# Attention and feed-forward block: the two 1024x1024 layers on 1024 tokens at a time instead of 512, after attention and the gated layer of all tokens

## The chip, the cores and the metric

The kernel runs on one core of one Trainium2 chip. The metric is device time in microseconds; the time shown is the median of three runs. A separate, profiled execution gives the trace that all the rows below come from. Its span runs from the first to the last instruction, and its own measured time is a little longer than its span.

## The reference, cut to what matters

Input x has 8 batches of 256 rows of 256 numbers; ctx has 120 rows of 256 for each batch.

```python
x = x + xattn(layernorm(x), ctx, ctx, ctx)     # h = gelu(xn @ ctx.T) * (xn @ ctx.T); h @ ctx
x = x + ffn(layernorm(x))

def ffn(x):                                    # weights are -1, 0 or 1, one scale per output column
    h = silu(tlin(x, w1)) * tlin(x, w2)        # 256 -> 1024, twice
    h = gelu(tlin(h, h1))                      # 1024 -> 1024
    h = gelu(tlin(h, h2))                      # 1024 -> 1024
    return tlin(h, w3)                         # 1024 -> 256
```

All numbers are 32 bit floats. There are 2048 token rows in all.

## The kernel before, in words

**Data.** Activations lie with features on the 128 partitions and tokens along the free side. A layer's 1024 features are two halves of 512 (four blocks of 128). The large operands are split into a rounded high part and a low part (the rest), both in the type float32r, so each product is done twice, once with each part. The weights are small integers and exact.

**Tokens.** The 2048 tokens are four groups of 512, t = 0 to 3; each has two batches (c = 0, 1).

**Attention** (class `Attention`, lines 179 to 278) works on one batch: layernorm (statistics L224, aggregates L228, epsilon L229, power -0.5 on GpSimd L232, normalization on VectorE L236), four transposes (L248), scores (L253), Gelu built from a square, a tanh and two VectorE steps (L266 to L271), values (L258), residual x1 (L274), a second layernorm, four transposes, and the split into xT high and low (L386, L387). It has three sets of buffers.

**Gated layer** (`gated`, L395): for each of eight feature blocks eight matmuls (L406), a Silu (L428) and a multiply (L430). For t = 0 it is done in two halves of 256 tokens, otherwise with 512-column matmuls.

**Hidden layers** (`hidden`, L470): a 1024x1024 layer on 512 tokens is treated as a 2x2 by 2x2 block product with seven block products instead of eight (Winograd's form of Strassen's method). The blocks of the activations are two feature halves by two batches, 512 features by 256 tokens each. `combine` (L473) forms the differences of blocks on VectorE, `operand` (L443) splits a block into high (ScalarE, L455) and low (VectorE, L459), and each product is 32 matmuls of 256 columns (L488). Sums of products are formed partly in PSUM, partly by copies (L508) and adds (L513), then Gelu (L498). Four of the seven weight blocks are loaded; `sum_weights` (L340) forms the sums.

**Stages.** Attention of batches 0 and 1 comes first; then, for each t, the gated layer and the first hidden layer, with the attention of the next group between the products. The results of the first layer for t = 0, 1, 2 go to DRAM (`spill`, L642) and are fetched again (L651) for the second layer, which runs for t = 3, 0, 1, 2, with the output layer (`output`, L543) of a finished group between the products of the next. Residual rows x1 of all batches stay in SBUF. The second layer's weights have tiles of their own, which take the place of the gated layer's weights. The last steps are row scaling and residual (L281, L282) and the transfer of 128 rows (L560).

**Check.** Each loaded weight is compared with its rounded form on the side: a Sign on ScalarE (L353), an accumulating transfer on GpSimd's queue (L355) and an OR on VectorE (L357). A flag selects a general path that this input doesn't take.

**Order.** All steps are put into a list with an engine, an estimated duration and the keys that they read and write. `Plan` orders them by a list schedule: the ready step with the longest remaining chain goes first, with ranks altered by random draws whose seeds are listed in `PICKS`. The order on each engine is then fixed in the program. Matmuls of the products stay in program order among themselves (chain "main"), as do those of the output ("out"), and the weight loads on GpSimd's queue ("weights"). Plain loads and stores go through SP's queue.

Of the kernel before, what the change touches and what calls it, by code (L numbers as in the profile page):

```python
# [20 lines left out]
P = 128  # L21
NB = 8
# [9 lines left out]
RING = 4  # L32

PICKS = (
    22, 45, 50, 74, 104, 131, 164, 176, 201, 234, 250, 272, 301, 336, 451, 637, 985, 1048, 1076,
    1087, 1162, 1188, 1253, 1293, 1302, 1322, 1348, 1410, 1437, 1496, 1527, 1586, 1637, 1766,
    1800, 1916, 2021, 2155, 2228, 2261, 2374, 2518, 2712, 2767, 2934, 2972, 3083, 3173, 3226,
    3393, 3456, 3487, 3595, 3625, 3738, 3967, 3987, 4030, 4260, 4277, 4303, 4438, 4471, 4529,
    4557, 4631, 4753, 4792, 4821, 5029, 5162, 5277, 5281, 5943, 6311, 6315, 6360, 6825, 6957,
    7038, 7141, 7325, 7506, 11104, 11302, 14059, 14203, 14339, 14562, 14820, 16005, 35431,  # L40
    35629, 36277, 36481, 37244, 38287, 38876, 40840, 40973, 59388, 59602, 59975, 60086, 60142,
    60267,
)
FORCE_GENERAL = False

# [10 lines left out]
GROUP = {2: "a", 1: "b", 6: "b", 7: "b", 4: "b", 5: "c", 3: "c"}  # L56
BANKS = {"a": (0, 1), "c": (2, 3), "b": (4, 5)}
OPENS, CLOSES = (1, 5, 2), (2, 3, 4)
ORDER = (1, 5, 2, 6, 3, 7, 4)
ORDER_FIRST = (1, 2, 5, 6, 3, 7, 4)  # L60
ORDER_NEXT = (1, 5, 6, 3, 7, 2, 4)
# [99 lines left out]
PE = 0.119  # L161
# [3 lines left out]
def xattn_ffn_kernel(ctx: ExitStack, tc: tile.TileContext, x, ctx_b, wall, scal, s3, out):  # L165
# [13 lines left out]
    class Attention:  # L179


        def __init__(self, pool, n):
            new = lambda name, shape: [pool.tile(shape, F32, name=f"{name}{i}") for i in range(n)]
            self.xb, self.cb = new("xb", [P, 2, D]), new("cb", [P, 2 * L + D])
            self.xn, self.xnT = new("xn", [P, 2, D]), new("xnT", [P, 2, S])
            self.e, self.q = new("ge", [L, S]), new("gq", [L, S])
            self.st, self.mv = new("ln_st", [P, 2, 6]), new("ln_mv", [P, 2, 2])
            self.ve, self.rs = new("ln_ve", [P, 2]), new("ln_rs", [P, 2])

        def load(self, plan, b, i, pieces):  # L190
            xv = x[b * S : (b + 1) * S, :].rearrange("(j p) d -> p j d", p=P)

            def load_x(js):
                nc.sync.dma_start(self.xb[i][:, js, :], xv[:, js, :])  # L194

            for js in pieces:
                plan.dma("SP", 0.45, lambda js=js: load_x(js), 0.128 * (js.stop - js.start),
                         lag=(2.2, 3.5)[b] if b < 2 else 8.0, w=[("xb", i, j) for j in range(js.start, js.stop)])
            plan.dma("SP", 0.45, lambda: nc.sync.dma_start(self.cb[i], ctx_b[b]), 0.25,
                     lag=2.5 if b < 2 else 8.0, w=[("cb", i)])  # L200

        def run(self, plan, b, i, js, bank, bank_key, x1, x1_key, finish, early):
# [6 lines left out]
            keys = lambda name: [(name, i, j) for j in blocks]  # L209
            xb, xn = self.xb[i][:, js, :], self.xn[i][:, js, :]  # L210
            cT = self.cb[i][:, : 2 * L].rearrange("p (k l) -> p k l", k=2)
            cN = self.cb[i][:L, 2 * L :]
            xnT, e, q = self.xnT[i][:, :, cols], self.e[i][:, cols], self.q[i][:, cols]
            st, mv = self.st[i][:, js, :], self.mv[i][:, js, :]
            ve, rs = self.ve[i][:, js], self.rs[i][:, js]
# [5 lines left out]
            def layernorm(src, src_keys, name):  # L221
# [4 lines left out]
                def aggregate():  # L226
                    for j in range(nj):
                        nc.vector.bn_aggr(mv[:, j, :], st[:, j, :])  # L228
                    nc.vector.tensor_scalar_add(ve, mv[:, :, 1], EPS)  # L229

                def root():
                    nc.gpsimd.tensor_tensor(rs, ve, eps_exp[:, :nj], op=ALU.pow)  # L232

                def norm():
                    for j in range(nj):
                        nc.vector.tensor_scalar(  # L236
                            xn[:, j, :], src[:, j, :], mv[:, j, 0:1], rs[:, j : j + 1],
                            op0=ALU.subtract, op1=ALU.mult)

                add("DVE", 0.42 * nj, stats, src_keys, keys("st"))  # L240
                add("DVE", 0.17 * nj + 0.15, aggregate, keys("st"), keys("mv"))
                add("POOL", 0.45 + 0.3 * nj, root, keys("mv"), keys("rs") + [(name, b, j) for j in blocks])
                add("DVE", 0.42 * nj, norm, src_keys + keys("mv") + keys("rs"), keys("xn"))
# [20 lines left out]
            add("PE", 0.43 * nj, scores, keys("xnT") + [("cb", i)], [bank_key])  # L264
# [8 lines left out]
            add("PE", 0.43 * nj, values, keys("e") + [("cb", i)], [bank_key])  # L273
# [11 lines left out]
    with ExitStack() as es, ExitStack() as wide:  # L285
# [4 lines left out]
        dram = open_pool(es, "spill", space=DRAM)  # L290
        es.enter_context(tc.manual_schedule())

        mm = [psum.tile([P, N], F32, name=f"mm{i}") for i in range(6)]
        pa = [psum.tile([P, N], F32, name=f"pa{i}") for i in range(2)]
        hi = [keep.tile([P, 4, S], F32R, name=f"hi{i}") for i in range(RING)]
        lo = [keep.tile([P, 4, S], F32R, name=f"lo{i}") for i in range(RING)]
        half = {n: keep.tile([P, 4, N], F32, name=n) for n in ("hb0", "hb1", "hc0", "hc1")}
        p1 = keep.tile([P, 4, S], F32, name="p1")
        u2 = keep.tile([P, 4, S], F32, name="u2")
        p5 = keep.tile([P, 4, S], F32, name="p5")  # L300
        x1 = keep.tile([P, 2 * NB, D], F32, name="x1")
        spill = dram.tile([NT, 2, P, 4 * N], F32, name="spill")

        first = es.enter_context(ExitStack())
        h1p = open_pool(first, "h1p")
        h1 = {n: h1p.tile([P, 4, 4, P], F32R, name=f"h1_{n}")
              for n in ("11", "12", "21", "22", "s1", "s2", "s4")}
        early_pool = open_pool(wide, "early", side="right")
        w12 = early_pool.tile([P, 4, 1024], F32R, name="w12")
        xT = [early_pool.tile([P, 2, N], F32R, name=f"xT{i}") for i in range(2)]  # L310
        att = Attention(early_pool, 3)

        def rings_of(pool, into):
            into["d"] = [pool.tile([P, 1024], BF16, name=f"d{i}") for i in range(4)]
            into["w32"] = pool.tile([P, 2, 512], F32, name="w32")

        sooner, later = {}, {}
        rings_of(early_pool, sooner)
# [10 lines left out]
        def load_layer(layer, blocks, order, gate=()):  # L329
            for name in order:  # L330
                plan.dma("POOL", 0.8, lambda name=name: nc.gpsimd.dma_start(
                    blocks()[name].rearrange("p m k c -> p m (k c)"), block_rows(layer, name)), 1.05 * (1 + 0.5 * layer),
                         r=gate, w=[("h", layer, name, m) for m in range(4)], chain="weights")

        def sum_weights(layer, blocks):
            for into, a, b, op in (("s1", "21", "22", ALU.add), ("s2", "s1", "11", ALU.subtract),
                                   ("s4", "12", "s2", ALU.subtract), ("21", "11", "21", ALU.subtract)):
                for m in range(4):
                    add("DVE", dve(512), lambda into=into, a=a, b=b, op=op, m=m:
                        nc.vector.tensor_tensor(  # L340
                            blocks()[into][:, m], blocks()[a][:, m].bitcast(F32),
                            blocks()[b][:, m].bitcast(F32), op=op),
                        r=[("h", layer, a, m), ("h", layer, b, m)], w=[("h", layer, into, m)])
# [3 lines left out]
        def check(of, tile, src, keys, rings, gate=()):  # L347

            d = lambda i=checks[0] % 4: rings()["d"][i]
            key = ("d", checks[0] % 4)  # L350
            checks[0] += 1
            d4 = lambda: d().rearrange("p (m c) -> p m c", m=src.shape[1])
            add("ACT", act(1024), lambda: nc.scalar.activation(  # L353
                d(), tile().bitcast(F32), AF.Sign, scale=-1.0), r=keys + list(gate), w=[key])
            plan.dma("POOL", 0.8, lambda: nc.gpsimd.dma_start(d4(), src, accum_op=ALU.add), 1.04,  # L355
                     w=[key], lag=8.0)
            add("DVE", 0.16 + 512 / 960, lambda: nc.vector.tensor_tensor(  # L357
                bad, bad, d(), op=ALU.logical_or), r=[key], w=["bad"])

        def check_block(layer, blocks, name, rings, gate=()):  # L360
            for m in (0, 2):
                src = block_rows(layer, name)[:, m : m + 2, :]
                if name != "21":
                    keys = [("h", layer, name, m), ("h", layer, name, m + 1)]
                    tile = lambda m=m: blocks()[name][:, m : m + 2].rearrange("p m k c -> p (m k c)")
                else:
                    keys = ["w32"]
                    tile = lambda: rings()["w32"].rearrange("p m c -> p (m c)")
                    plan.dma("SP", 0.45, lambda src=src: nc.sync.dma_start(rings()["w32"], src), 0.52,
                             r=gate, w=["w32"], lag=6.0)  # L370
                check(name, tile, src, keys, rings, gate)

        def check_chunk(c, tile, keys, rings, gate=()):
            check(c, tile, wall[c : c + 1].rearrange("c p f -> p c f"), keys, rings, gate)


        def attention(b, pieces, banks, early):
            t, c, i = b // 2, b % 2, b % 3
            att.load(plan, b, i, pieces)
            for js, (bank, key) in zip(pieces, banks):  # L380
                cols = slice(c * S + js.start * P, c * S + js.stop * P)
                xkey = [("xT", c, j) for j in range(js.start, js.stop)]

                def finish(p, bank_key, n, early, cols=cols, xkey=xkey):
                    hi, lo = (v[:, :, cols] for v in xT)
# [402 lines left out]
```

## Time and profile before

| | |
|---|---|
| median of 3 runs | 350.26 us (349.5 to 350.3) |
| profiled execution, its own time | 350.58 us |
| its span | 348.8 us |
| TensorE, VectorE, ScalarE, GpSimd busy | 331.8, 266.0, 224.0, 46.9 us |
| hidden products, share of the chain | 61.2% (1792 matmuls of 256 columns) |
| gated layer, share of the chain | 17.2% (192 of 512 columns, 128 of 256) |
| output layer, share of the chain | 8.6% (256 of 256 columns) |

In the chain of work that ended last each piece has its start, its duration, its engine, the tile that it writes, its line and the number of instructions. In the groups a row has the line, the engine, the operation, the tiles and shapes, the count, the busy time, the mean duration of one and the idle time before it. A matmul's own duration in such a row (284 ns with 256 columns) includes time that overlaps with the next one; what one costs in a dense stretch is the stretch divided by its count.

### The profile page before, as it was taken

To read this page: it belongs to the slowest core of one execution; us is meant where nothing else is said; L and a number is where in the kernel's file an instruction comes from. 1 tells how busy PE (TensorE), PEld (TensorE's weight loads), DVE (VectorE), ACT (ScalarE), POOL (GpSimd) and SP (SyncE) were. 2 spreads that over 40 slices of the span, in tenths; PEclk is the share of its full clock that TensorE was granted. 3 is DMA by queue.
4 is the path that set the end of the run, shared out by engine and by line. 5 is a ranking of instruction groups with operands and counts; after the bars stand their busy time and mean duration, and the time that the engine had idled before them with its cause. 6 is when DMAs were issued, how large, how long until landed. Compare 5 with 4: busy or idle time off the path is not lost.

```text
span 348.8 us, 6241 instructions
## 1 busy us (share of the span) xinstructions
PE 331.8 (95%) x2502; PEld 317.7 (91%) x2502; DVE 266.0 (76%) x440; ACT 224.0 (64%) x360; POOL 46.9 (13%) x57
## 2 busy tenths in 40 slices
PE   3799999999999999999999999999999999999991
PEld 2499999888999889999899999999999999999991
DVE  4779998878988678952598998999499846895551
ACT  2339566697974968456585588989487636854540
POOL 5411000261423100000040005105000000000000
PEclk9999999999999999999999999999999999999998
DMA  7992001599596620004149917715780006000011
GB/s 201 375 381 81 2 0 34 150 291 156 47 138 62 185 85 2 2 2 165 77 131 400 314 62 79 116 19 56 94 274 32 1 17 257 15 17 31 20 43 37
DMA packets 19042, 38.81 MB, mean 111 GB/s; under 512 B 1472, under 2 KB 10816, under 8 KB 17472
## 3 DMA queue, kind: packets, MB, share of 16 engines
q0 software_dynamic: 10256, 17.30, 26.9%
q1 hardware_dynamic: 8752, 21.06, 16.9%
q8 instruction: 21, 0.34, 0.4%
q14 instruction: 13, 0.11, 0.1%
HBM read 35.73 MB, written 8.39 MB: 126 GB/s over the span
## 4 chain that ended last, share of the span: by engine, by line
PE 94%; DVE 2%; DMA 1%; ACT 1%; issue 0%; SPq 0%
PE mm L488 61%; PE mm L406 17%; PE pa L543 9%; PE pa L258 2%; PE pa L253 2%; PE pa L248 2%; DMA sc<-scal_d 1%; PE mm L258 1%; PE mm L253 1%; DVE xT L387 0%; DVE o L281 0%; PE mm L248 0%; SPq L194 0%; DVE gq L267 0%; ACT ge L266 0%
## 5 line engine op out<-in xcount | busy, mean ns | idle before, releaser
L488 PE MATMUL mm<-hi,h 128*128 128x256 f32 x512 | 72.4, 284 | 0.0
L488 PE MATMUL mm<-lo,h 128*128 128x256 f32 x512 | 71.4, 282 | 0.0
L488 PEld LDWEIGHTS mm<-hi,h 128*128 128x128 f32 x512 | 65.7, 190 | 0.5 <-ACT hb L428 0.3
L488 PEld LDWEIGHTS mm<-lo,h 128*128 128x128 f32 x512 | 65.6, 190 | 0.0
L406 PE MATMUL mm<-xT,w 128*128 128x512 f32 (+1 forms) x320 | 63.0, 355 | 0.8 <-ACT xT L386 0.7
L406 PEld LDWEIGHTS mm<-xT,w 128*128 128x128 f32 x320 | 52.2, 194 | 9.1 <-ACT xT L386 1.0
L459 DVE TENSOR_TENSOR lo<-hb,hi 128x1024 fp32r<-128x1024 f32 (+2 forms) x47 | 52.5, 1129 | 7.6 <-ACT hi L455 7.4
L488 PE MATMUL mm<-hi,h_s 128*128 128x256 f32 x384 | 54.2, 284 | 0.0
L488 PE MATMUL mm<-lo,h_s 128*128 128x256 f32 x384 | 53.5, 282 | 0.0
L455 ACT CAST hi<-hb 128x1024 fp32r<-128x1024 f32 (+2 forms) x47 | 45.3, 975 | 7.5 <-issue 2.5
L488 PEld LDWEIGHTS mm<-hi,h_s 128*128 128x128 f32 x384 | 49.3, 190 | 0.2
L488 PEld LDWEIGHTS mm<-lo,h_s 128*128 128x128 f32 x384 | 49.2, 190 | 0.0
L498 ACT ACTIVATE hc<-hc,sc 128x256 f32<-128x256 f32 x60 | 27.3, 504 | 15.8 <-DVE hc L513 15.8
L355 POOL DMA_DIRECT2D d<-wall_d x22 | 24.8, 1141 | 93.3 <-ACT d L353 90.9
L430 DVE SCALAR_TENSOR_TENSOR hb<-hb,sc,mm 128x512 f32<-128x512 f32 (+1 forms) x40 | 25.1, 637 | 13.9 <-ACT hb L428 9.9
L428 ACT ACTIVATE hb<-mm,sc 128x512 f32<-128x512 f32 (+1 forms) x40 | 23.7, 604 | 15.2 <-PE mm L406 15.0
L232 POOL TENSOR_TENSOR ln_rs<-ln_ve,eps_exp 128x2 f32<-128x2 f32 (+1 forms) x18 | 13.8, 798 | 92.5 <-DVE ln_ve L229 51.8
L508 ACT COPY p<-mm 128x512 f32<-128x512 f32 x32 | 18.5, 585 | 10.0 <-PE mm L488 9.6
L459 DVE TENSOR_TENSOR lo<-hc,hi 128x1024 fp32r<-128x1024 f32 x18 | 21.8, 1219 | 2.5 <-ACT hi L455 2.5
L455 ACT CAST hi<-hc 128x1024 fp32r<-128x1024 f32 x18 | 18.8, 1048 | 4.9 <-DVE hb L513 2.3
L543 PE MATMUL pa<-w,hi 128*128 128x256 f32 x128 | 21.5, 281 | 0.4 <-DVE o L281 0.4
L543 PE MATMUL pa<-w,lo 128*128 128x256 f32 x128 | 21.1, 279 | 0.0
(85 smaller groups left out, 387.7 us busy)
## 6 DMA issues: line engine op xcount, KB each, us to landing
h<-wall_d POOLq DMA_DIRECT2D x8, 1024.0 KB, 14.6
spill<-hc SPq DMA_DIRECT2D x6, 1024.0 KB, 4.3
d<-wall_d POOLq DMA_DIRECT2D x22, 256.0 KB, 5.9
w<-wall_d POOLq DMA_DIRECT2D x3, 1024.0 KB, 9.9
w<-wall_d SPq DMA_DIRECT2D x4, 512.0 KB, 4.3
hd<-spill SPq DMA_DIRECT2D x2, 1024.0 KB, 8.2
out_d<-o SPq DMA_DIRECT2D x16, 128.0 KB, 1.7
hb<-spill SPq DMA_DIRECT2D x2, 1024.0 KB, 5.4
```

Source lines behind the costliest of these rows:

```text
L232: nc.gpsimd.tensor_tensor(rs, ve, eps_exp[:, :nj], op=ALU.pow)
L253: nc.tensor.matmul(g, lhsT=cT[:, k, :], rhs=xnT[:, k, :], start=(k == 0), stop=(k == 1))
L355: plan.dma("POOL", 0.8, lambda: nc.gpsimd.dma_start(d4(), src, accum_op=ALU.add), 1.04, w=[key], lag=8.0)
L406: nc.tensor.matmul(sides[side], lhsT=w12[:, m // 2, (((m % 2) * 2 + side) * 2 + k) * P :][:, :P], rhs=xT[i][:, k, cols], start=first and ( ...
L428: add("ACT", act(n), lambda o=o, b0=b0, m=m: nc.scalar.activation(o, b0, AF.Silu, scale=sc[:, m : m + 1]), r=[("mm", banks[0]), "sc", "tab ...
L430: add("DVE", dve(n) - 0.03, lambda o=o, b1=b1, m=m: nc.vector.scalar_tensor_tensor(o, o, sc[:, 8 + m : 9 + m], b1, op0=ALU.mult, op1=ALU.m ...
L455: nc.scalar.copy(views()[0], src())
L459: nc.vector.tensor_sub(l, src(), h.bitcast(F32))
L488: nc.tensor.matmul(bank[:, m * S : (m + 1) * S], lhsT=w[:, 2 * b + m, k, :], rhs=part[:, k, :], start=(p in OPENS and part is hi[slot] and ...
L498: return lambda: nc.scalar.activation(o(), o() if src is None else src, AF.Gelu, scale=sc[:, col : col + 1])
L508: add("ACT", act(512), lambda: nc.scalar.copy(flat(to, b), bank2(i)), r=[key], w=[(name, b)])
L543: nc.tensor.matmul(pa[j][:, :D], lhsT=part[:, k, j * P : (j + 1) * P], rhs=later["w3"][:, r, k * D : (k + 1) * D], start=(r == 0 and k == ...
```

## The change

- `hidden` works on 1024 tokens: its blocks are 512 features by 512 tokens, a pair of groups (t = 0, 1, then t = 2, 3). A product is 32 matmuls of 512 columns over four PSUM banks; there are four calls in place of eight. Copies and adds still work on 512 columns; a Gelu now has 512 columns instead of 256. Calls take turns with the two sets of four banks.
- Attention and gated layer of all four groups run before the first hidden layer. t = 0 and t = 1 are done in halves (`HALVED`). The gated layer takes turns over banks 0 to 4, attention over 5 to 7. xT is there twice, and there are four sets of load buffers. From batch 2 on the normalization runs on ScalarE, with one more small step on VectorE and one on GpSimd (`NORM_ON_ACT`).
- Activations stay in SBUF (eight tiles q of 512 features by 512 tokens, and two more once the first operand's tile is free). The residual x1 goes to DRAM (`x1s`) and comes back for the output.
- Layer 1's weights load into layer 0's tiles (`HOME`) as these become free; layer 0's load after batch 4's first normalization. Operands have three slots instead of four, of double size. Operands are split in two pieces of 1024 elements per partition.
- The output of the four groups follows the last hidden call, with four PSUM banks and all 512 tokens at a time.
- Checks of layer 0 and of the gated weights start after the gated stage; the gated weights are fetched again for theirs.
- The Silu table is loaded once, and the Gelu table once. `PICKS` are other seeds.

The diff, cut to its core:

```diff
-RING = 4
+RING = 3
...
+HALVED = 2
+NORM_ON_ACT = 2
...
-BANKS = {"a": (0, 1), "c": (2, 3), "b": (4, 5)}
-OPENS, CLOSES = (1, 5, 2), (2, 3, 4)
-ORDER = (1, 5, 2, 6, 3, 7, 4)
...
+ORDER = (1, 2, 5, 6, 3, 7, 4)
+IN_X = (1, 6, 7, 4)
+OPENS, CLOSES = (1, 2, 5), (2, 3, 4)
+
+HOME = (
+    {"11": 0, "12": 1, "21": 2, "22": 3, "s1": 4, "s2": 5, "s4": 6},
+    {"21": 0, "22": 1, "s1": 4, "11": 5, "s2": 6, "12": 2, "s4": 3},
+)
...
 def root():
     nc.gpsimd.tensor_tensor(rs, ve, eps_exp[:, :nj], op=ALU.pow)
+    if on_act:
+        nc.gpsimd.tensor_tensor(sh, nm, rs, op=ALU.mult)
...
+                        if on_act:
+                            nc.scalar.activation(xn[:, j, :], src[:, j, :], AF.Identity,
+                                                 scale=rs[:, j : j + 1], bias=sh[:, j : j + 1])
...
+                plan.dma("SP", 0.45, lambda js=js, x1=x1: nc.sync.dma_start(
+                    x1s[b * S : (b + 1) * S, :].rearrange("(j p) d -> p j d", p=P)[:, js, :], x1),
...
+            def product(p, slot, m, bank):
+                w = weight(layer, WEIGHT[p])
+                for kind, part in enumerate(slot_views(slot)):
+                    for k in range(4):
+                        nc.tensor.matmul(
+                            mm[bank], lhsT=w[:, m, k, :], rhs=part[:, k, :],
+                            start=(p in OPENS and kind == 0 and k == 0),
+                            stop=(p in CLOSES and kind == 1 and k == 3), skip_group_check=True)
...
+            for p in ORDER:
                 if p in make:
                     combine(*make[p])
+                slot = operand(where[p], first and p == 1)
+                if p == 6:
+                    combine(b21, b21, b11)
+                for m in range(4):
+                    bank = (X if p in IN_X else Y)[m]
...
+        gated(0, 0)
+        gated(0, 1)
+        for t in range(1, NT):
+            for b in (2 * t, 2 * t + 1):
+                attention(b, both, (5 + (b + 1) % 3,), 6.0)
+            for c in (0, 1) if t < HALVED else (None,):
+                gated(t, c)
+        load_layer(0, ("11", "12", "21", "22"), [("first", 4, 0)])
+        sum_weights(0, (S1, S2, S4, S3))
...
+        blocks[0], spare = hidden(0, blocks[0], spare, low, high, first=True)
...
+        blocks[1], spare = hidden(0, blocks[1], spare, high, low)
+        load_layer(1, ("21", "22", "11", "12"))
+        sum_weights(1, (S1, S2, S3, S4))
+        blocks[0], spare = hidden(1, blocks[0], spare, low, high)
...
+        blocks[1], spare = hidden(1, blocks[1], spare, high, low)
+        (c11, c12, c21, c22), (e11, e12, e21, e22) = blocks
+        output(0, c11, c21, low)
+        output(1, c12, c22, high)
+        output(3, e12, e22, low)
...
+        output(2, e11, e21, high)
```

## The prediction

> **What bounds the kernel now.** I read the busy shares first, then the chain that ended last, then that chain in order of time, and last the groups of the stage that the change rearranges.
>
> ```profile
> PE 331.8 (95%) x2502; PEld 317.7 (91%) x2502; DVE 266.0 (76%) x440; ACT 224.0 (64%) x360; POOL 46.9 (13%) x57
> ...
> PE 94%; DVE 2%; DMA 1%; ACT 1%; issue 0%; SPq 0%
> PE mm L488 61%; PE mm L406 17%; PE pa L543 9%; PE pa L258 2%; PE pa L253 2%; PE pa L248 2%; DMA sc<-scal_d 1%; PE mm L258 1%; PE mm L253 1%; DVE xT L387 0%; DVE o L281 0%; PE mm L248 0%; SPq L194 0%; DVE gq L267 0%; ACT ge L266 0%
> ```
>
> TensorE is 94% of the chain, so only two things can move the end: TensorE's own instruction time, and the few places where it waits. The chain in order of time shows both:
>
> ```profile
> 5.57 1.12 PE mm L248 x4
> ...
> 19.68 7.53 PE mm L406 x56
> ...
> 67.44 0.02 issue
> 67.46 0.47 ACT hc L498
> 67.94 0.56 ACT xT L386
> 68.49 0.02 issue
> 68.51 1.30 DVE xT L387 x2
> 69.81 0.04 issue
> 69.86 5.40 PE mm L406 x22
> ...
> 163.08 14.53 PE mm L406 x64
> 177.62 66.76 PE mm L488 x560
> ...
> 337.37 3.76 PE pa L543 x30
> 341.13 0.02 issue
> 341.15 0.44 DVE o L281
> ```
>
> From 19.7 to 341.1 us TensorE hardly stops. The waits are 67.44 to 69.86 (2.4 us: the gated layer of t=1 waits for the transposed rows xT) and 336.78 to 337.37 (0.6 us, before the last piece). Ahead of 19.7 lie the first loads and the attention of batches 0 and 1; behind 341.13 lie two output blocks on VectorE (1.7 us) and the last transfer.
>
> **Part 1, the products (the gain).** Seven products per call stay seven, and the columns that stream are the same: 8 calls x 224 matmuls of 256 columns become 4 calls x 224 of 512. So 1792 x 256 columns become 896 x 512, and what changes is the cost per instruction. For 256 columns the chain gives 61.2% of 348.8 = 213.5 us for 1792, or 119.1 ns each (66.76/560 = 119.2 in the long stretch). For 512 columns the gated layer has the same data type and row count: 14.53/64 = 227.0 ns. New time 896 x 227.0 = 203.4 us, **10.1 us less**. Here a rule speaks against the change: the Trainium skill, TensorE: Matmul & The Clock Gate, section on the 56 ns gap, puts the fixed cost of a warm matmul at about 2.5 ns beyond its columns. By it, 896 instructions fewer save 2.2 us only. This case's rows say 2 x 119.1 - 227.0 = 11.2 ns per pair, and two uninterrupted stretches beside each other carry it, so I take the rows; the rule's sum becomes a rival.
>
> **Part 2, gated layer and output.** All four 512-token groups now run first, and t=1 is split in halves as t=0 was: 64 matmuls of 512 become 128 of 256, 128 x 119.1 - 64 x 227.0 = **+0.7 us**. The output keeps 256 matmuls of 256 columns (0). Attention's TensorE work is unchanged (2.6 us per batch warm: four transposes twice 0.87, scores 0.86, values 0.87).
>
> **Part 3, what VectorE and ScalarE lose and gain.** Off the path while TensorE has work. ScalarE: 128 Gelus of 256 (63.5 us by their rows: 0.504 from SBUF, 0.47 from PSUM) become 64 of 512; the copy's step from 256 to 512 columns is 0.587 - 0.372 = 0.215 us, so about 0.70 each, 44.8 us: -19. Table loads: 10 x 1.28 become about two: -10. The normalization of batches 2 to 7 moves from VectorE (24 x 0.405 = 9.7 us) to ScalarE; the nearest row, an ACTIVATE on 256 elements with a scale column, is 0.504, so +12. VectorE gets 12 small negations (0.17, +2) instead. GpSimd gets 12 tiny products behind its powers: between 0.2 us (its small fill) and 0.86 (its power on 128x2); I take 0.5, twice per batch in a chain of 15 us or more, hidden while rows of another batch are ready. Operand splits, subtractions and PSUM adds keep their elements. Of transfers, 6 MB of spill and as much of reload go; 2 MB of x1 is stored and fetched instead. On SP an x1 store waits for VectorE, and the x load of a later batch stands behind it; four load buffers cover this. If not, a load of 4.4 us is late by the store's wait.
>
> **Part 4, the new first stage (the price).** Work that was spread between products now stands together. Per batch TensorE needs 2.6 for attention and 7.6 for the gated half: 10.2 us (9.9 with 512 columns). VectorE: two layernorms (statistics 0.83, aggregates 0.32, two small ones 0.34) 3.0, the four others 0.42 + 0.42 + 0.69 + 0.68, in all 5.2 (6.5 for batches 0 and 1), plus eight gated multiplies at 0.476 = 3.8, or 3.0 as half of eight at 0.744. ScalarE: 2.0 + 2.0 + 3.8 = 7.8. So TensorE stays the slowest, but VectorE has 8.2 to 10.3 of 10.2. The stage ends on TensorE at 19.1 + 59.9 of gated (128 x 227.0 + 256 x 119.1 = 59.5, 0.4 for the first slow ones) + 16.0 of attention = 95 us. VectorE's total in it: 13.0 + 30.9 + 15.2 + 11.9 = 71.0, with the first operand 2.4 and layer 0's sixteen weight sums (0.683 each, 10.9), 84.3. It reached 91% from 20 to 60 us (36.5 of 40), at which this ends at 2.8 + 84.3/0.91 = 95.4: level with TensorE, and half of the sums may slip into the first product call, where VectorE has 35 us (14 splits and 8 subtractions at 1.22, 12 adds at 0.68) in 51. Depth: batch 1 needed from 7.5 (first statistics) to 29.0 (xT low part), 21.5 us; with three sets of buffers and three PSUM banks that is one batch per 7.2 us, under 10.2. So the bounds are 0 and the loss of before's corresponding stretch, where 19 to 75 us lost 0.9 (56 matmuls in 7.53 instead of 6.67), 2.4 and 0.4 (22 in 5.40), 3.7 us. I take **4**, nearer that end because the margins of VectorE are thin, and book the 2.4 us wait as removed. Layer 0's weights now load after batch 4's first normalization: four issues of 0.77 us on GpSimd, behind which a power can stand 3.1 us, and 4 MB that need about 11 us (1 MB of layer 1 landed in 11.0 median with five together) against 40 available: 0.
>
> **Part 5, layer 1's weights into layer 0's tiles.** They can only load as the second call's products release them. The last, block 12, goes where block 21 was and waits for the sixth product. Then the seventh product and the next call's first one cover 2 x 32 x 0.227 = 14.5 us. Issue 0.8 plus landing 5.6 (fastest 1 MB) to 11.0: covered. Uncovered only at the worst landing, 19.4 (queued behind 4 MB): 5.7 us. The sums wait on these loads but are used from the third product on. I take 0. On GpSimd check transfers wait behind a held weight load; only the flag waits for those.
>
> **Part 6, the end.** Outputs now run after the last product: 4 x 7.6 = 30.3 us on TensorE, VectorE 28.2 of it (12 of 16 splits at 1.22, 16 x 0.85 row finishes): fits, thinly; three operand slots release in time. The 0.6 us wait goes. Only one block instead of two remains after the last matmul: -0.8.
>
> **Sum** against the profiled execution: 348.8 - 10.1 + 0.7 - 2.4 - 0.6 - 0.8 + 4.0 = 339.6 span; 1.8 lies around it (350.58 - 348.8), 341.4; the profiled run is 0.3 above the median of 350.26, so **341.1 us**.
>
> **Rivals.**
> 1. *The 512-column matmul saves only the rule's 2.2 us.* Then 349.0, inside 0.3% of before (about what a measurement of this kernel can tell from no change). The 227.0 row speaks against it. 5%.
> 2. *The first stage starves TensorE (slower).* One mechanism: a batch's long chain of small steps over three engines paces the stage. It gives rows every chain/3; over 10.2 us TensorE waits, and six batches times the excess eats the gain of 9.2 when the excess is 1.5 us beyond the 4 already booked /6, that is 12.4 us per batch or a chain of 37 us. A chain of 40 gives 13.3, 18.6 in place of 4: 356. For it: VectorE's thin margin, fixed orders per engine, and a rule of the same page (clock gate): idle windows of about 3.4 us halve the array's clock. The trace shows the start like that (four score matmuls 2.07 us at 13.28, 0.86 later), though its granted clock says 1.00. Against it: 21.5 us for batch 1, with loads contending. 11%, 8% slower than before.
> 3. *The weight reload is late*, 2 to 5.7 us: 343 to 347. 9%.
> 4. *The stage loses nothing*: 337. 12%.
>
> The forecast, 338.5 to 344, has the remaining 63%. Faster than before by over 0.3%: 63 + 9 + 12 + 2 of rival 2 = 86%; within: 5 + 1 = 6%; slower 8%. The range 337.0 to 347.5 leaves out most of rivals 1 and 2 and the fringe of 4.
>
> **What would show it.** Hidden products 227 ns apart, 203 us in the chain; the gated stage's last matmul at 93 to 97 us; no TensorE wait of over 1 us at the layer change; about 30 us of output without a wait. Wrong if products come above 232 ns, or TensorE waits sum above 8 us before 100 us.

## The result and the profile after

The changed kernel takes 345.11 us (median, 344.32 to 345.15) against 350.28 us before, a ratio of 0.985 (95% interval 0.983 to 0.987). It is 5.2 us faster; 9.2 were forecast. The profiled execution took 345.08 us, with a span of 343.0.

First the shares and the chain of the changed kernel:

```profile
PE 325.9 (95%) x1670; PEld 274.8 (80%) x1670; DVE 261.4 (76%) x432; ACT 215.2 (63%) x316; POOL 50.0 (15%) x69
...
PE 93%; DVE 2%; DMA 2%; SPq 1%; issue 0%; DVEq 0%
PE mm L511 61%; PE mm L429 17%; PE mm L562 9%; PE mm L274 2%; DMA xb<-x_d 2%; PE mm L264 2%; PE mm L269 2%; DVE ln_st L232 1%; SPq L205 1%; SPq L199 0%; DVE xb L290 0%; DVE o L297 0%; DVE xn L252 0%; DVE ge L287 0%; DVE o L298 0%
```

TensorE is still the chain, in nearly the same shares; L511 are the hidden products, L429 the gated layer, L562 the output. The chain in order of time has only two large pieces after the first stage, one of hidden products and one of output (start, duration, what):

```profile
19.80 1.19 PE mm L429 x8
...
64.10 0.02 issue
64.12 0.69 DVE xb L290
64.81 0.34 DVE ge L287
65.16 0.04 issue
65.20 1.13 PE mm L274 x4
...
76.33 19.99 PE mm L429 x88
96.32 208.86 PE mm L511 x896
305.18 28.79 PE mm L562 x240
```

From 96.32 to 305.18 there is not one wait, at the layer change either. The first stage waits once, 1.1 us at 64.1. So nothing that I had feared came about, and still the kernel is 4 us behind the forecast: 208.86/896 is **233.1 ns per 512-column matmul**, where the gated layer in the line above it has 19.99/88 = 227.2. The 6 ns are the whole question. The products went from 213.5 to 208.9 us, 4.6 less instead of 10.1.

The groups of the stretch in which the first product runs (96.2 to 103.4 us) hold a clue: this product is the one whose operand lies in two tiles of its own, op0 (high and low part).

```profile
L511 PE MATMUL mm<-op,w 128*128 128x512 f32 x32 | 7.4, 389 | 0.0
```

The mean of one is 389 ns (overlaps included); for the other products the page has

```profile
L511 PE MATMUL mm<-hi,w 128*128 128x512 f32 x432 | 118.4, 395 | 0.0
L511 PE MATMUL mm<-lo,w 128*128 128x512 f32 x432 | 118.4, 395 | 0.0
```

Same code line, same pool of weight tiles, same shape: what differs is the tile that streams. By the starts in the trace, matmuls from op0 follow each other at 226.8 ns, those from hi and lo at 233.3, from the second product of the first call to the last of the last, in a fixed rhythm of 234, 231, 235, 233 over the four blocks k. Load on the other engines comes and goes in that time; a rhythm tied to the block number suggests addresses.

The addresses are in the built program. The weights start at byte 73664 of each partition, op0 at 143296, the gated weights at 161344 and xT at 177728: all multiples of 64. The pool that holds hi, lo and w3 is filled from the top of the memory, and its tiles start at 162784 (hi), 187360 (lo) and 211936 (w3): 32 beyond a multiple of 64. The kernel before mixed them too: hi, lo and layer 0's weights at multiples of 64, layer 1's weights and w3 at 32 beyond. Its own chain (before), in pieces of layer 0 and of layer 1 that the prediction lumped together, reads 119.8 and 118.3 ns for 256 columns:

```profile
134.50 15.34 PE mm L488 x128
...
302.79 7.57 PE mm L488 x64
```

### The profile page after: what moved, and what is told of

The parts are those of the page before. It is cut to its first block, busy times and chain, and to the rows that moved or that the text cites. A ratio compares the mean times of both kernels' runs of the same rounds, so it can differ in the third digit from the quotient of the medians.

```text
span 343.0 us, 4574 instructions
## 1 busy us (share of the span) xinstructions
PE 325.9 (95%) x1670; PEld 274.8 (80%) x1670; DVE 261.4 (76%) x432; ACT 215.2 (63%) x316; POOL 50.0 (15%) x69
## 4 chain that ended last, share of the span: by engine, by line
PE 93%; DVE 2%; DMA 2%; SPq 1%; issue 0%; DVEq 0%
PE mm L511 61%; PE mm L429 17%; PE mm L562 9%; PE mm L274 2%; DMA xb<-x_d 2%; PE mm L264 2%; PE mm L269 2%; DVE ln_st L232 1%; SPq L205 1%; SPq L199 0%; DVE xb L290 0%; DVE o L297 0%; DVE xn L252 0%; DVE ge L287 0%; DVE o L298 0%
## 5 line engine op out<-in xcount | busy, mean ns | idle before, releaser
L511 PE MATMUL mm<-hi,w 128*128 128x512 f32 x432 | 118.4, 395 | 0.0
L511 PE MATMUL mm<-lo,w 128*128 128x512 f32 x432 | 118.4, 395 | 0.0
L484 DVE TENSOR_TENSOR lo<-q,hi 128x1024 fp32r<-128x1024 f32 x70 | 83.8, 1220 | 21.3 <-ACT hi L480 21.3
L511 PEld LDWEIGHTS mm<-lo,w 128*128 128x128 f32 x432 | 81.0, 187 | 19.8
L511 PEld LDWEIGHTS mm<-hi,w 128*128 128x128 f32 x432 | 80.9, 187 | 19.8
L480 ACT CAST hi<-q 128x1024 fp32r<-128x1024 f32 x70 | 70.1, 1045 | 9.7 <-PE mm L562 7.9
L429 PE MATMUL mm<-xT,w 128*128 128x256 f32 (+1 forms) x384 | 65.2, 325 | 0.0
L429 PEld LDWEIGHTS mm<-xT,w 128*128 128x128 f32 x384 | 56.4, 191 | 5.3
L526 DVE TENSOR_TENSOR q<-q,mm 128x512 f32<-128x512 f32 x48 | 32.9, 687 | 26.8 <-PE mm L511 26.0
L530 ACT ACTIVATE q<-q,sc 128x512 f32<-128x512 f32 x48 | 34.4, 723 | 27.0 <-DVE q L526 27.0
L503 DVE TENSOR_TENSOR q<-q,q 128x1024 f32<-128x1024 f32 x32 | 38.1, 1219 | 0.0
L562 PE MATMUL mm<-w,hi 128*128 128x256 f32 x128 | 20.7, 284 | 0.0
L562 PE MATMUL mm<-w,lo 128*128 128x256 f32 x128 | 20.6, 283 | 0.0
L562 PEld LDWEIGHTS mm<-w,hi 128*128 128x128 f32 x128 | 17.7, 192 | 0.1
```

The costliest lines, as they stand in the source:

```text
L429: nc.tensor.matmul(sides[side], lhsT=w12[:, m // 2, (((m % 2) * 2 + side) * 2 + k) * P :][:, :P], rhs=xT[t % 2][i][:, k, cols], start=firs ...
L480: nc.scalar.copy(slot_views(i)[0][:, ms], q[src][:, ms])
L484: nc.vector.tensor_sub(l[:, ms], q[src][:, ms], h[:, ms].bitcast(F32))
L503: add("DVE", dve(1024), lambda ms=ms: nc.vector.tensor_tensor(q[into][:, ms], q[x][:, ms], q[y][:, ms], op=ALU.subtract), r=q_keys(x, ms) ...
L511: nc.tensor.matmul(mm[bank], lhsT=w[:, m, k, :], rhs=part[:, k, :], start=(p in OPENS and kind == 0 and k == 0), stop=(p in CLOSES and kin ...
L526: add("DVE", dve(512), lambda: nc.vector.tensor_tensor(o(), o(), mm[bank], op=ALU.add), r=[key], w=[("q", i, m)])
```

## The experiments

**Theory A**: what a matmul costs depends on whether its moving operand (the one that streams) and its stationary operand (the one loaded into the array, here the weights) start in the same half of a 64-byte line. "Line" is a name for 64 bytes counted from address 0; the width of 64 is part of the theory. **Theory B**: only the moving operand's own start counts. **Rival C**: the traffic of VectorE and ScalarE, or the clock, slows TensorE in the hidden stage, wherever the tiles lie.

In the first group each edit is one unused tile of 32 bytes. The runs of the kernel before on that chip had a median of 348.38 us, so ratios count. The times of one kernel's executions differ by some us, in part with TensorE's clock at the start (see the last run below); the pieces of hidden products lie in a stretch with a granted clock of 1.00, so they carry the argument.

*Operands 32 bytes lower.*

```diff
             later["x1"] = [pool2.tile([P, D], F32, name=f"x1_{i}") for i in range(6)]
+            pool2.tile([P, 8], F32, name="pad")
```

> All tiles of the pool with hi, lo and w3 lie 32 bytes lower, so hi, lo and w3 start at a multiple of 64 bytes, as the weights do; nothing else changes. Theory A (place: a 512-column matmul costs 6.5 ns more when its moving operand starts in another half of a 64-byte line than its stationary one): hidden products fall from 233.1 to 227 ns, 5.6 us less, about 339.5 us. Theory B (the moving operand's own place counts): the same here. Rival C (VectorE's and ScalarE's traffic, or the clock, slows TensorE in the hidden stage): 233 ns and 345.1 us stay.

Measured: 339.65 us, ratio 0.972 (0.964 to 0.981). The chain:

```profile
97.12 203.10 PE mm L511 x896
300.22 28.79 PE mm L562 x240
```

203.10/896 = 226.7 ns: 5.8 us gone from the products by moving tiles 32 bytes. Over this stage VectorE and ScalarE were as busy as in the changed kernel (from 97.1 to 300.2 us here, 96.3 to 305.2 there), and the granted clock was 1.00 in both. The first row is the changed kernel's, the second this one's:

```profile
96.30:305.20 208.90, 208.90 (x899) 167.97 (x898) 156.55 (x175) 147.61 (x192) 27.71 (x26) 1.00 0.39 66
```

```profile
97.10:300.20 203.10, 203.10 (x899) 168.18 (x898) 155.75 (x175) 147.49 (x192) 27.71 (x26) 1.00 0.40 68
```

The columns are the stretch, its length, busy time of TensorE, weight loads, VectorE, ScalarE and GpSimd, the clock, the DMA share and GB/s. VectorE did 155.75 us of work in the stretch, against 156.55, in less time. Rival C is out as the cause of the 6 ns.

*The same, but w3 stays.* The unused tile stands before w3 instead of behind x1.

```diff
+            pool2.tile([P, 8], F32, name="pad")
             later["w3"] = pool2.tile([P, 2, 1024], F32R, name="w3")
```

> As the kernel with hi, lo and w3 shifted by 32 bytes, but w3 stays where it was, half a line from hi and lo. Theory A: hidden products 227 ns as there; the output's 256-column matmuls, whose two operands now start in different halves, go from 119.9 to about 117 ns as in the kernel before (hi, lo at 0 and w3 at 32 there): 0.75 us less again, about 338.8 us. Theory C: 345.1.

Measured: 337.85 us, ratio 0.968 (0.961 to 0.975). The output, whose stationary operand is hi or lo and whose moving one is w3, went from 28.79 to 28.00 us for 240 matmuls (120.0 to 116.7 ns):

```profile
96.41 203.10 PE mm L511 x896
299.50 28.00 PE mm L562 x240
```

*Weights 32 bytes higher instead.*

```diff
+        keep.tile([P, 8], F32, name="padk")
         wt = [keep.tile([P, 4, 4, P], F32R, name=f"w{i}") for i in range(7)]
```

> The changed kernel with the seven weight tiles (and what lies behind them on the left side) 32 bytes higher, hi and lo unchanged at 32: both operands start at 32. Theory A: same half, so 227 ns and about 339.5 us. Theory B (own place of the moving operand): 233 ns, 345.1 us. Rival C: 345.1 us.

Measured: 338.83 us, ratio 0.971 (0.966 to 0.977), products 226.7 ns. Hi and lo lie where they lay in the changed kernel. Theory B is out: the two operands' places relative to each other count.

```profile
97.33 203.14 PE mm L512 x896
```

*Both edits.*

> Weights at 32, hi and lo at 0: different halves, the other way round than in the changed kernel. Theory A: 233 ns, about 345 us (the first product, whose operand moved with the weights, stays at 227). Theory B: 227 ns, 339.5 us. Rival C: 345.1 us.

Measured: 344.2 us, ratio 0.985 (0.979 to 0.992), as the changed kernel; products 233.3 ns, and the first product, whose operand moved along with the weights, 227.9.

```profile
95.93 208.90 PE mm L512 x896
```

**Width against placement.** In the second group the hidden products go back to 256 columns, at both placements (median before on that chip: 349.27 us).

```diff
                 for kind, part in enumerate(slot_views(slot)):
+                    for h in range(2):
+                        cols = slice(h * S, (h + 1) * S)
                         for k in range(4):
                             nc.tensor.matmul(
-                                mm[bank], lhsT=w[:, m, k, :], rhs=part[:, k, :],
+                                mm[bank][:, cols], lhsT=w[:, m, k, :], rhs=part[:, k, cols],
```

> The changed kernel with each hidden product done in 256-column matmuls again (1792 instead of 896, both halves with a weight load of their own), operands where they are (hi, lo at 32, weights at 0). Theory A (256 columns: 120 ns in the same half of a line, 117 to 118 in different halves; 512: 227 and 233): hidden products 1792 x 117.5 = 210.6 us against 208.9, so about 347 us: at this placement the wide matmul saves under 2 us. The prediction's rate (119.1 for 256): 213.4, about 349.6.

Measured: 346.69 us, ratio 0.992 (0.989 to 0.995).

```profile
97.20 211.20 PE mm L513 x1792
```

> 256-column hidden products and hi, lo, w3 32 bytes lower, in the same half of a line as the weights. Theory A: 1792 x 119.9 = 214.9 us against 203.1 with 512 columns at the same placement, 11.8 us more, about 351 us. If 256 columns cost the same at both placements: as the run with 256 columns at the old placement.

Measured: 350.09 us, ratio 1.002 (1.000 to 1.005).

```profile
97.10 215.04 PE mm L513 x1792
```

Together, in ns per matmul of the hidden products:

| | same half of a line | different halves | the first costs |
|---|---|---|---|
| 256 columns | 120.0 | 117.9 | +2.1 |
| 512 columns | 226.7 | 233.1 | -6.4 |
| two of 256 less one of 512 | 13.3 | 2.7 | |

These are averages over the whole stage; the column of different halves has the first product in it, whose operands lie in the same half (without it 117.8 and 233.3).

The preference turns round with the width. At the changed kernel's own placement the wide matmul saves 211.2 - 208.9 = 2.3 us of products; in the same half it saves 215.0 - 203.1 = 11.9. Without the wide matmuls, the rest of the change gains nothing over the kernel before with both operands in the same half (ratio 1.002), and 0.8% with different halves (0.992).

**The normalization on VectorE**, to test the thin margin of the first stage:

```diff
-NORM_ON_ACT = 2
+NORM_ON_ACT = 8
```

> The changed kernel with all normalizations on VectorE again (24 more steps of 0.405 us there, 12 negations of 0.185 fewer; 24 steps of 0.59 fewer on ScalarE, 12 products of 0.335 fewer on GpSimd), every step in the same plan. If VectorE's thin margin in the first stage decides (prediction, part 4): 7.5 us more VectorE work in that stage, which ends 3 to 7.5 us later than 96.3, 348 to 352 us. If VectorE still has room there: within 1 us of 345.1.

Measured: 346.44 us, ratio 0.990 (0.986 to 0.993), against 0.985 for the changed kernel elsewhere. The interval ends at 347.8 us on the scale of the forecast (0.993 of 350.28), just under its 348 to 352; the middle, 1.5 us above the changed kernel, lies outside the 1 us as well. In the profiled execution the gated layer even ended earlier than in the changed kernel's, at 95.18:

```profile
54.31 0.58 ACT xnT L279
...
56.96 0.69 DVE xb L290
57.66 0.40 DVE q L452
...
73.39 21.80 PE mm L429 x96
95.18 208.86 PE mm L511 x896
```

But this execution is no typical one. At 342.97 us it is the fastest of the eight, with a mean granted clock of 0.996; six of the others have 0.983 to 0.987 and 346.4 to 347.0 us. Its early end comes with a granted clock of 1.00 from 17 to 20 us, where the changed kernel's trace has 0.50. VectorE was busy for 70.7 of the 77.2 us from 19.1 to 96.3, against 66.4 with the normalization on ScalarE, and TensorE waited longer: from one matmul to the next 0.7 us for the step of the first row and 1.2 us for those of the next two, 1.8 us in all against the single wait of 1.1. The same edit on the version with hi and lo shifted and w3 not:

> hi and lo 32 bytes lower, w3 not, and all normalizations on VectorE. If VectorE's margin in the first stage doesn't decide: within 1.2 us of the version with the normalization on ScalarE (337.9 there, 0.968 of before), in either direction; if it does: 3 us or more slower than that.

Measured: 339.23 us, ratio 0.972 (0.967 to 0.977), 1.5 us or so above that version's 0.968, with intervals that overlap. That lies between the two forecasts. This profiled execution (339.21 us) is a typical one, and its hidden products begin at 98.03 us, against 96.41 in the trace of the version with the normalization on ScalarE:

```profile
57.15 0.58 ACT xnT L279
...
59.80 0.69 DVE xb L290
60.49 0.40 DVE q L452
...
98.03 203.10 PE mm L511 x896
```

The two waits are there again, 1.8 us against 1.1, which is 0.7 of the 1.6 us. With them goes a clock that came later: 0.50 granted from 20 to 22 us and 0.83 to 24, where the other trace has 1.00. So all normalizations on VectorE cost TensorE about 0.7 us of waits in both pairs of traces, far from 3 to 7; whether the later clock belongs to the edit or to chance stays open.

**The kernel before, with layer 0's weights moved**:

```diff
         h1p = open_pool(first, "h1p")
+        h1p.tile([P, 8], F32, name="padh")
```

> The kernel before with layer 0's seven weight tiles 32 bytes higher, in another half of a line than its hi and lo, as layer 1's weights already are there. Theory A: layer 0's 896 matmuls of 256 columns go from 119.8 to 118.3 ns, 1.4 us less than the kernel before. Otherwise no change.

Measured: 347.31 us, ratio 0.995 (0.993 to 0.997). Layer 0's matmuls start 118.3 ns apart instead of 119.8; the long stretch went from 66.76 us to

```profile
176.05 66.41 PE mm L489 x560
```

Of the measured 2.0 us (interval 1.0 to 2.4) the placement accounts for 1.4.

**The changed kernel again, and another pair of tiles** (median before: 349.37 us). The third group repeats the changed kernel and moves the gated weights against xT, on top of shifted hi and lo:

> The changed kernel itself, beside the two below on one chip: 233.1 ns per hidden matmul, ratio to before 0.985.

Measured: 343.74 us, ratio 0.983 (0.979 to 0.987), 233.1 ns.

```diff
+        early_pool.tile([P, 8], F32, name="padx")
         xT = [[early_pool.tile([P, 2, N], F32R, name=f"xT{i}{j}") for i in range(2)] for j in range(2)]
```

> hi and lo 32 bytes lower, w3 not, and the gated weights 32 bytes lower too, so that the gated layer's two operands lie in different halves of a line. Theory A for another pair of tiles: its 128 matmuls of 512 columns go from 226.7 to 233 ns (+0.8 us), its 256 of 256 columns from 120 to 118 (-0.5 us where TensorE doesn't wait); the time stays within 0.5 us of 337.9. If the effect belonged to the hidden stage alone: 227 and 120 ns stay.

Measured: 337.06 us, ratio 0.965 (0.961 to 0.969), the fastest version, but no proof of a gain over 0.968. The gated layer's 512-column matmuls went to 20.53/88 = 233.3 ns, its 256-column ones to 5.61/48 = 116.9 (in the changed kernel 5.75/48 = 119.8), as theory A has it. The first row is the changed kernel's:

```profile
27.42 5.75 PE mm L429 x48
```

```profile
24.93 5.61 PE mm L430 x48
...
73.46 20.53 PE mm L430 x88
93.99 203.13 PE mm L512 x896
297.12 28.00 PE mm L563 x240
```

This profiled execution began its gated layer at 17.65 us instead of 19.80. That is mostly the clock, not placement. In the same stretch from 17 to 20 us TensorE's granted clock was 0.50 in the changed kernel's execution (first row) and 1.00 in this one (second):

```profile
17.00:20.00 3.00, 3.00 (x11) 2.53 (x11) 1.85 (x8) 0.53 (x2) 0.90 (x2) 0.50 0.11 32
```

```profile
17.00:20.00 3.00, 3.00 (x24) 2.83 (x23) 2.28 (x8) 2.21 (x5) 1.45 (x3) 1.00 0.45 134
```

The ten matmuls just ahead of the gated layer took 3.3 us there and 1.9 here. The changed kernel's chain also runs through one slow transfer of x (`5.04 6.57 DMA xb<-x_d`), but the version with only hi and lo shifted began at 20.13 us without one, at a clock of 0.50 too. Times go with this clock in some kernels: of the 20 executions with 256 columns and shifted operands, the two with a mean granted clock of 0.999 took 347.9 and 348.0 us, the four with 0.986 took 351.1 to 351.6. In the version with the weights shifted they don't (0.998 at 339.4 us, 0.990 at 338.3); its trace has slow matmuls at the start (four of L274 in 1.72 us, against 1.03 here) although the recorded clock says 1.00. So differences of a microsecond or two between two spans are not read as effects here.

## Why the prediction was right or wrong

The direction, the bound and the range were right; the time was 4.0 us too low. That it fell into the range is partly luck. It lies above the forecast's own 338.5 to 344, where room had been left for a late weight reload (rival 3) that did not happen, and an error of 2.7 us in the first stage hid part of the 6.2 us missing elsewhere. By the prediction's own sign, "wrong if products come above 232 ns", its main term was wrong: they came at 233.1. In the terms of its sum:

- **Part 1, the products: the step that failed.** The size was off: 10.1 us forecast, 4.6 measured. The reading was the error: the prediction took 227.0 ns from the gated layer because it had "the same data type and row count", and took for granted that nothing else about the tiles matters. It matters where they start. At equal halves the row holds to 0.3 ns (226.7). The 119.1 for 256 columns was an average over two placements as well, 119.8 and 118.3; both pieces stood in the chain that it read. Missing here: +5.5 us.
- **The rule that was set aside.** By the Trainium skill, TensorE: Matmul & The Clock Gate, "Wait — 56ns, not 53.3ns?", 2.2 us would be saved; with widths compared at the placement of the changed kernel the run has 2.3. That is a coincidence, since the placement moves the two widths in opposite directions, and no confirmation of a fixed 2.5 ns: at equal halves the same comparison has 11.9 us, 13.3 ns for each matmul saved. Rival 1 came halfway true by another mechanism than its own.
- **Part 2.** The output was booked at nothing. It went from 117.0 to 119.9 ns per matmul, since hi and lo moved into the half in which w3 lies: +0.7 us.
- **Part 4, the first stage.** Its TensorE work was to end at 95 us, and I added 4 for waits. It ended at 96.3: 0.7 more from the later start and 1.1 from the one wait, 0.5 less because attention took 15.5 us instead of the 16.0 in the sum (six times its own 2.6 is 15.6). For this stage rival 4, no loss, was nearer than the forecast. VectorE was busy for 86% of the stage, and even with all normalizations on it (92%) TensorE waited only 0.7 us more; a thin margin had been counted as a loss. -2.7 us. Nothing of the size of rival 2 was seen.
- **Part 5, the weight reload: right.** The last block was issued at 193.57 us and landed at 199.27, in 5.7 us; the third call begins at about 201 and needs it at its second product, about 208. Nine microseconds were to spare, and rival 3 is out.
- **Part 6: right.** The output has no wait. From the last matmul's end to the end of the span it took 6.8 us, against 7.5 before.
- **Part 3: right where it counted.** The normalization on ScalarE took 0.592 us instead of 0.504, the Gelu 0.69 to 0.72 for 0.70, the small product on GpSimd 0.335 for 0.5.

The sum with these terms: 339.6 + 5.5 + 0.7 - 2.7 = 343.1 against a span of 343.0.

## What to carry to other kernels

A duration taken from another line of the same kernel is only as good as the likeness of its operands, and their addresses are part of that. Compare starts per instruction between tiles before averaging them: a step of a few ns on a few hundred matmuls is several microseconds where TensorE is the chain. When a kernel's tile sizes change, look at where the large operands start; an unused tile of 32 bytes is a cheap trial. Here it was worth about as much as the whole change: 0.965 to 0.972 instead of 0.983 to 0.985. And before a profiled execution is set against another, look at the granted clock of both and at where each lies among its kernel's times.

## What the runs showed of the hardware that I had not expected

A float32r matmul at a granted clock of 1.00, with a weight load for each, took 226.7 ns for 512 columns where the starts of moving and stationary operand were equal modulo 64 bytes, and 233.1 where they differed by 32; for 256 columns it was the other way round, 120.0 and 117.9. It was seen with hidden products, output and gated layer, and whichever operand was moved. Other offsets than 32 weren't tried. In every pair of tiles measured here the two starts differ by a multiple of 512 bytes, or by 32 more or less than one, so that the pattern repeats every 64 bytes is not shown. Why the sign changes with the width stays open too: the runs show that it is the relative place, not what arbitrates.
